# Adding both experts' results of a token in the DRAM row by the indirect store itself

## The chip, the cores and the metric

One core of one Trainium2 chip runs the whole program. The metric is the time on the device in microseconds (us) of one execution; timed runs are taken without the profiler, and beside them one execution was recorded by the hardware profiler. A core has five engines with queues of their own: PE (matrix products; PEld is its weight load), DVE (VectorE), ACT (ScalarE), POOL (GpSimd) and SP (SyncE, which here only issues transfers). Sixteen DMA engines move the data.

## The reference

Sixteen sequences of 256 tokens with 256 features (4096 tokens) go through two layers. What matters here is the last part, the second layer's feed-forward: attention, and then a mixture of eight experts, of which each token takes two.

```python
x = x + o @ w_o + b_o
h = _layernorm(x, ln2_g, ln2_b).reshape(B * S, D)
logits = h @ gate_w + gate_b
topv, topi = jax.lax.top_k(logits, TOPK)            # TOPK = 2
gw = jax.nn.softmax(topv, axis=-1)
ew = jnp.sum(jax.nn.one_hot(topi, E, dtype=h.dtype) * gw[..., None], axis=1)
hid = jax.nn.relu(jnp.einsum('td,edf->etf', h, W1) + b1[:, None, :])
out_e = jnp.einsum('etf,efd->etd', hid, W2) + b2[:, None, :]
moe = jnp.einsum('etd,te->td', out_e, ew)
return x + moe.reshape(B, S, D)
```

Ahead of it stand, in this order: a first layer's mixture of experts (with a shared one), a product-key memory of 4096 experts, and an LSTM over the 256 steps, whose output is the input of the attention. The result of the last part is added to that of the product-key stage.

## The kernel before

The program is one long instruction stream for each engine; a scheduler orders it when the kernel is built, from the dependences between tiles and DRAM tensors, and may move an instruction ahead of others in the source. Each engine runs its own list strictly in that order. There are three stages.

**The first stage** (0 to about 446 us) computes the first layer. Its experts' results go by indirect stores to the DRAM tensor `ayd`, one row for each of a token's two choices. `join` loads both rows of 128 tokens into `r` (L222, on SP), adds them on POOL (L224), turns them by PE (L227) and adds them to `y` on DVE (L229). The last of it overlaps the setup of the next stage: loads of `wx` and `wh` (L973, L974) and of `h0` (L975), scalings of both weights on POOL (L995, L996), memsets.

**The product-key stage** (to about 2345 us) goes over 32 steps `u` of 128 tokens; it has one round more, for the LSTM, which runs one step behind. Each round selects experts on DVE (`select_experts`, which reads `yt`, loaded by L724), builds weights, multiplies by the tables (L839 and L865 on PE) and runs eight LSTM steps (`recur`, L933). `inputs_of` stores the LSTM's inputs to the DRAM tensor `xwd` (L898) and `load_inputs` reads them back (L902). The loads and stores of this stage are on SP.

**The last stage** runs attention of one sequence after another (`front`, `heads`, `ends`) and, interleaved with it by a fixed plan, the experts in 71 tiles of 128 rows (NTL). `ends` finds each token's two experts and sends its row, with the gate and the number of the result's row behind it, to the DRAM tensor `xsd`, in the expert's own region (L1414 on POOL, indirect). The number comes from `dest_i`: choice `c` of token `t` has the number `c * N + t`. After the last sequence, eight `fill` rows of 128 (L1429) close the regions: they have the gate 0 and the numbers from 2N on, a dump of 128 rows.

`experts` then works on tile `n` in three rounds of its loop. `load_tile` loads the rows `xs`, the expert's `w1`, `b1` and `b2` (L1486 to L1495, all on SP). `turn_in` transposes the rows (L1501) and copies them to `xT` (L1503, ACT). `first` is the first product (L1513, PE) with its bias and ReLU in eight pieces, by turns on DVE (L1519) and ACT (L1517). `second` is:

```python
for f in range(NF):
    m = nc.tensor.matmul(acc, hT[n][:, f], mw2[...e...], start=(f == 0), stop=(f == NF - 1))   # L1526
ys = eg.tile([P, D], F32, name="ys", bufs=3)
nc.vector.scalar_tensor_tensor(ys, acc, xs[n][:, D : D + 1], b2[n], ALU.mult, ALU.add)       # L1531
to = eg.tile([P, 1], U32, name="to", bufs=3)
nc.vector.tensor_copy(to, xs[n][:, D + 1 : W].bitcast(U32))                                  # L1533
nc.gpsimd.indirect_dma_start(out=ysd, out_offset=bass.IndirectOffsetOnAxis(ap=to, axis=0), in_=ys, in_offset=None)
```

The last line is L1534: the 128 results go to the rows `to` of the DRAM tensor `ysd`, which has 2N + 128 rows. Nothing in the source says that these stores are independent, so each one waits on POOL for the one before. `to` and `ys` have three buffers each.

After the last attention the tiles that remain follow each other without a break. Eight tiles before the end of the program's loop the source starts to load `base0` to `base7` (L1600 on SP, 512 KB each): the sum so far, kept by `ends` in the DRAM tensor `x3d`. At the end, `ysd` is read back in eight blocks of 512 tokens:

```python
r = jx.tile([P, 2, UB, D], F32, name="r", bufs=4)
for w in range(2):
    at = w * N + c * TBLK
    nc.sync.dma_start(out=r[:, w], in_=ysd[at : at + TBLK].rearrange("(u p) d -> p u d", p=P))   # L1608
nc.vector.tensor_tensor(r[:, 0], r[:, 0], r[:, 1], ALU.add)                                      # L1609
```

Four times two transposes (L1613) and an addition to `base` (L1614) each follow, and the store of the block to `out` (L1615, on ACT's queue).

Of the kernel before, what the change touches and what calls it, by code (L numbers as in the profile page):

```python
# [8 lines left out]
F32 = mybir.dt.float32  # L9
# [3 lines left out]
ALU = mybir.AluOpType  # L13
# [4 lines left out]
P = 128  # L18
B, T, D = 16, 256, 256
N = B * T  # L20
# [13 lines left out]
TBLK = 512  # L34
# [13 lines left out]
def steps(gen, n=None):  # L48

    while n is None or n > 0:  # L50
        if next(gen, gen) is gen:
            return
        n = None if n is None else n - 1
# [108 lines left out]
def adaln_ffn_kernel(ctx: ExitStack, tc: tile.TileContext, i: dict, out: bass.AP):  # L162
    nc = tc.nc
# [3 lines left out]
    ident = const.tile([P, P], F32, name="ident")  # L167
# [7 lines left out]
    pid_i = const.tile([P, 1], mybir.dt.int32, name="pid_i")  # L175
# [15 lines left out]
    I32 = mybir.dt.int32  # L191
# [4 lines left out]
    W = D + 2  # L196
# [41 lines left out]
    with (  # L238
# [70 lines left out]
        dest_i = aw.tile([P, 2, NU], I32, name="dest_i")  # L309
# [260 lines left out]
        with tc.issue_after(marks[1]):  # L570
            nc.scalar.dma_start(out=gam, in_=i["gamma"])
            nc.scalar.dma_start(out=bet, in_=i["beta"])
            for q in range(2):
                w = NE // 2
                nc.scalar.dma_start(out=kin[:, :, q * w : (q + 1) * w], in_=i["kinT"][:, :, q * w : (q + 1) * w])
        with tc.issue_after(marks[2]):
            for q in range(2):
                w = NC // 2
# [55 lines left out]
    NCH = T // SPC  # L634
# [8 lines left out]
    with tc.tile_pool(name="cw", bufs=1) as cw:  # L643
# [8 lines left out]
        dram2 = ctx.enter_context(tc.tile_pool(name="dram2", bufs=1, space=DRAM))  # L652
# [2 lines left out]
        NID = E * (CAP + 1)  # L655
        W = D + 2
        xsd = dram2.tile([(NID + 1) * P, W], F32, name="xsd")
        ysd = dram2.tile([2 * N + P, D], F32, name="ysd")
        x3d = dram2.tile([P, KC, N], F32, name="x3d")
        QC = AH * 32 // P  # L660

# [12 lines left out]
        wh = cw.tile([P, KC, 4, D], F32, name="wh")  # L674
        h0 = cw.tile([P, KC, B], F32, name="h0")
        lnw = fw.tile([P, 4, KC], F32, name="w_ln")
        z0 = fw.tile([P, KC, T], F32, name="z0")
        wqk = fw.tile([P, 2, KC, D], F32, name="wqk")
        with (
# [29 lines left out]
            def tiles_of(c):  # L709
                return slice(c * XT * SPC, (c + 1) * XT * SPC)  # L710
# [3 lines left out]
            def of_tile(ap, u):  # L714
                return ap[:, :, :, u * SPC : (u + 1) * SPC]
# [184 lines left out]
            def load_inputs(v, half):  # L900
                for j in range(CG):
                    nc.sync.dma_start(  # L902
                        out=xr[half][j * CW : j * CW + B],
                        in_=xwd[v].rearrange("(t b) j f -> j b t f", b=B)[j, :, half * HS2 : (half + 1) * HS2],
                    )
# [50 lines left out]
            def new_w():  # L956
                return cx.tile([P, NC, P], F32, name="wts")
# [7 lines left out]
            w = new_w()  # L965
# [15 lines left out]
            for n, gate in enumerate(ORDER):  # L981
                for k in range(KC):
                    at = gate * KC + k
# [26 lines left out]
            def chosen_by(u):  # L1010

                if u < 0:
                    return 0
                return min((NCH - 1) * NS, NS * (u + 1) + min(NS, NS // 4 * u))
# [10 lines left out]
            for u in range(NCH + 1):  # L1025
                if u < NCH:
                    if u % XT == 0:
                        xt[u // XT] = cx.tile([P, KC, B, XT * SPC], F32, name="x1", bufs=2)
                        nc.sync.dma_start(out=xt[u // XT], in_=i["xT"].rearrange("p k (b t) -> p k b t", t=T)[:, :, :, tiles_of(u // XT)])
                    part = of_tile(xt[u // XT], u % XT)  # L1030
                    dense = experts(u, w, part, early if u == 0 else None)

                at, must, to = chosen_by(u - 1), NS * (u + 1), chosen_by(u)
                lead = -(-max(0, must - at) // 2)
                gw = iter(())
                if u + 1 < NCH:
                    w = new_w()
                if u > 0:
                    v = u - 1
                    inputs_of(v, of_tile(xt[v // XT], v % XT))  # L1040
                    load_inputs(v, 0)
                    if v % XT == 0:
                        zt[v // XT] = cx.tile([P, KC, B, XT * SPC], F32, name="zt", bufs=2)
                    back = recur(v, of_tile(zt[v // XT], v % XT))
                NQ = NC // CQ
                for q in range(NQ):
                    if u < NCH:
                        steps(dense, 1)
                    if u + 1 < NCH:
                        if q < lead:  # L1050
                            steps(choices, min(2, must - at))
                            at += min(2, must - at)
                        else:
                            if q == lead:
                                gw = weights_of(done[u + 1], w)
                            n, of = q - lead, NQ - lead
                            steps(gw, (n + 1) * NQ // of - n * NQ // of)
                            more = (to - at) * (n + 1) // of - (to - at) * n // of
                            steps(choices, more)
                    steps(back, 1)  # L1060
                steps(back)
                steps(dense)
                steps(gw)
                if u < NCH and u % XT == XT - 1:
                    nc.sync.dma_start(out=x1d[:, :, :, tiles_of(u // XT)], in_=xt[u // XT])
                if u > 0 and v % XT == XT - 1:
                    nc.gpsimd.tensor_copy(z0[:, :, tiles_of(v // XT)], zt[v // XT][:, :, 0])
                    nc.sync.dma_start(out=zd[:, :, :, tiles_of(v // XT)], in_=zt[v // XT])
# [11 lines left out]
    I32 = mybir.dt.int32  # L1080
    final = ctx.enter_context(ExitStack())
    with (
# [25 lines left out]
        for m in range(2 * HC):  # L1108
            to, at = slice(m * DK, (m + 1) * DK), slice(m % HC * 32, m % HC * 32 + DK)
# [47 lines left out]
            nc.gpsimd.memset(t, 1.0)  # L1157
        fill = fl.tile([P, W], F32, name="fill")
        nc.gpsimd.memset(fill, 0.0)
        nc.vector.tensor_scalar(fill[:, D + 1 : W].bitcast(I32), pid_i, 2 * N, None, ALU.add)  # L1160
        nc.sync.dma_start(out=xsd[NID * P : (NID + 1) * P], in_=fill)
        NPAD = 2
        npads = fl.tile([P, NPAD, NTT, P], F32, name="npads")
# [22 lines left out]
        ecap = fl.tile([P, E], F32, name="ecap")  # L1186
        nc.vector.tensor_scalar(ecap, iota8, float(N + P), None, ALU.mult)
        dest_i = fl.tile([P, 2, N // P], I32, name="dest_i")
        nc.gpsimd.iota(dest_i, pattern=[[N, 2], [P, N // P]], base=0, channel_multiplier=1)

        count = fl.tile([P, E], F32, name="count0")
        nc.vector.memset(count, 0.0)
# [282 lines left out]
        def experts():  # L1475
# [45 lines left out]
            def second(n):  # L1521
                with tc.issue_after(done[n - 2]) if n > 1 else nullcontext():
                    e = nc.tensor.value_load(reg[n][0:1, n : n + 1], min_val=0, max_val=E - 1)
                acc = pg.tile([P, NF // 2, P], F32, name="g", tag="g").rearrange("p f n -> p (f n)")[:, 0:D]
                for f in range(NF):
                    m = nc.tensor.matmul(  # L1526
                        acc, hT[n][:, f], mw2[:, bass.ds(e, 1), f].rearrange("p o d -> p (o d)"), start=(f == 0), stop=(f == NF - 1)
                    )
                done[n] = m.ins
                ys = eg.tile([P, D], F32, name="ys", bufs=3)  # L1530
                nc.vector.scalar_tensor_tensor(ys, acc, xs[n][:, D : D + 1], b2[n], ALU.mult, ALU.add)  # L1531
                to = eg.tile([P, 1], U32, name="to", bufs=3)
                nc.vector.tensor_copy(to, xs[n][:, D + 1 : W].bitcast(U32))  # L1533
                nc.gpsimd.indirect_dma_start(out=ysd, out_offset=bass.IndirectOffsetOnAxis(ap=to, axis=0), in_=ys, in_offset=None)  # L1534

            for n in range(NTL + 2):
                if n < NTL:
                    load_tile(n)
                if 0 <= n - 1 < NTL:
                    turn_in(n - 1)  # L1540
                if n - 2 >= 0:
                    second(n - 2)
                yield
                for half in range(2):
                    if 0 <= n - 1 < NTL:
                        first(n - 1, half)
                    yield
# [45 lines left out]
        UB = 4  # L1593
        jx = final.enter_context(tc.tile_pool(name="jx", bufs=1))
        pj_ = final.enter_context(tc.tile_pool(name="jp", bufs=3, space=PSUM))
        base = []
# [5 lines left out]
        go(NTL * PIECES)  # L1602
        steps(moe)
        for c in range(NBLK):
            r = jx.tile([P, 2, UB, D], F32, name="r", bufs=4)
            for w in range(2):
                at = w * N + c * TBLK
                nc.sync.dma_start(out=r[:, w], in_=ysd[at : at + TBLK].rearrange("(u p) d -> p u d", p=P))  # L1608
            nc.vector.tensor_tensor(r[:, 0], r[:, 0], r[:, 1], ALU.add)  # L1609
            for u in range(UB):  # L1610
                pj = pj_.tile([P, KC, P], F32, name="pj")
                for k in range(KC):
                    nc.tensor.transpose(pj[:, k], r[:, 0, u, k * P : (k + 1) * P], ident)  # L1613
                nc.vector.tensor_tensor(base[c][:, :, u * P : (u + 1) * P], base[c][:, :, u * P : (u + 1) * P], pj, ALU.add)  # L1614
            nc.scalar.dma_start(out=out[:, :, c * TBLK : (c + 1) * TBLK], in_=base[c])  # L1615
# [77 lines left out]
```

## Time and profile before

| What | us |
|---|---|
| timed runs (3): median, lowest, highest | 3600.56, 3600.42, 3603.99 |
| the profiled execution's own time | 3588.3 |
| its span, from the first to the last instruction | 3585.7 |
| PE busy | 3371.2 (94%) |
| DVE busy | 2277.3 (64%) |
| ACT busy | 1494.7 (42%) |
| POOL busy | 682.5 (19%) |
| loads of `r` from `ysd` (L1608): 16 of 512 KB, median from issue to landing | 9.4 |
| additions of the two halves of `r` (L1609): 8, mean of one | 1.22 |
| indirect stores to `ysd` (L1534): 71, median on POOL; median to landing | 1.026; 2.5 |

A line of a timeline gives the start, the duration, the engine, the line of the kernel, the operation, the tiles as written <- read, their shapes and the count; in brackets stands the idle time of the engine just before, and what ended it. An engine name with a q (SPq) is the engine's own queue: the time in which it issues a transfer or waits for a semaphore. "DMA to landing" is counted from the issue to the moment at which the data have landed.

### The profile page before, as it was taken

The numbers are of one execution on the slowest core, as the hardware profiler recorded it, in microseconds if no ns is written. First come the engines' busy times: TensorE is split into PE (matmuls) and PEld (weight loads), VectorE is DVE, ScalarE is ACT, GpSimd is POOL, SyncE is SP. The second block draws the span as 40 slices with busy tenths as digits, with TensorE's granted clock in tenths as the row PEclk, the third lists the DMA queues.
The fourth block names the chain that finished last, engine by engine and source line by source line (L and its number), as shares of the span: only waits on it lengthen the run. The fifth ranks groups of instructions, "written<-read, shape, count | busy, mean of one in ns | idle before, by whom it ended". The sixth has DMA issues, their size and how long they took to land.

```text
span 3585.7 us, 72808 instructions
## 1 busy us (share of the span) xinstructions
PE 3371.2 (94%) x26776; PEld 2563.4 (71%) x26776; DVE 2277.3 (64%) x7358; ACT 1494.7 (42%) x3701; POOL 682.5 (19%) x1164
## 2 busy tenths in 40 slices
PE   8899979999999999999999999969999999999896
PEld 5377557777777777777777777735677777777796
DVE  4333478888878787878888787435555555564323
ACT  1133134545454454545454554334444434443221
POOL 4555210100010100000010100101222222222221
PEclk9899989999999999999999999968999999999997
DMA  6333521111111111011111111130223333333566
GB/s 229 124 103 101 175 41 31 19 34 22 36 24 29 36 23 37 16 37 22 36 22 31 33 23 31 28 120 21 74 92 114 104 117 104 117 102 102 195 216 222
DMA packets 422255, 272.78 MB, mean 76 GB/s; under 512 B 304720, under 2 KB 381136, under 8 KB 411024
## 3 DMA queue, kind: packets, MB, share of 16 engines
q1 hardware_dynamic: 397504, 207.95, 20.9%
q0 software_dynamic: 13344, 36.60, 2.8%
q10 hardware_dynamic: 11056, 23.60, 2.0%
q8 instruction: 216, 3.54, 0.4%
q14 instruction: 135, 1.11, 0.1%
HBM read 191.62 MB, written 76.44 MB: 75 GB/s over the span
## 4 chain that ended last, share of the span: by engine, by line
PE 77%; DVE 9%; ACT 4%; DMA 4%; issue 3%; POOL 2%; SPq 1%; ACTq 0%; DVEq 0%; POOLq 0%
PE acc L865 13%; PE po L839 9%; PE gp L933 7%; PE wp L822 7%; PE g L1526 6%; PE g L1513 6%; PE sc L1277 3%; PE sp L736 3%; PE bp L889 3%; PE ph L529 2%; PE mm L1305 2%; PE py L543 2%; DVE i L747 2%; DVE s L746 1%; PE acc L427 1%
## 5 line engine op out<-in xcount | busy, mean ns | idle before, releaser
L839 PEld LDWEIGHTS po<-yt,kin 128*128 128x128 f32 x3840 | 459.1, 191 | 104.4 <-issue 103.5
L865 PEld LDWEIGHTS acc<-ge,kout 128*128 128x128 f32 x3968 | 466.5, 192 | 85.7 <-DVE ge L862 42.2
L865 PE MATMUL acc<-ge,kout 128*128 128x128 f32 x3968 | 505.3, 280 | 3.1 <-DVE ge L862 1.7
L839 PE MATMUL po<-yt,kin 128*128 128x128 f32 x3840 | 507.0, 281 | 0.0
L826 ACT COPY wts<-wp 64x256 f32<-64x256 f32 x1024 | 375.2, 366 | 180.9 <-PE wp L822 168.2
L952 POOL TENSOR_SCALAR zt<-hT 128x32 f32<-128x32 f32 x256 | 122.4, 478 | 1552.3 <-DVE hT L951 1437.9
L933 PE MATMUL gp<-wh,hT 128*32 128x256 f32 x4096 | 318.3, 393 | 31.1 <-DVE hT L951 20.8
L817 DVE TENSOR_TENSOR oh<-chosen,parted 128x1024 f32<-128x1024 f32 x256 | 311.9, 1218 | 0.0
L822 PE MATMUL wp<-oh,ol 128*64 128x128 f32 x4096 | 297.4, 281 | 5.7 <-ACT wts L826 5.1
L1517 ACT ACTIVATE hT<-g,b 128x128 f32<-128x128 f32 x284 | 104.7, 369 | 423.9 <-DVE hT L1519 370.6
L1526 PE MATMUL g<-mw,hT 128*128 x1136 | 273.2, 396 | 5.6 <-ACT xT L1503 3.1
L1513 PE MATMUL g<-xT,w 128*128 128x128 f32 x2272 | 274.4, 276 | 1.0 <-DVE ys L1531 1.0
L1513 PEld LDWEIGHTS g<-xT,w 128*128 128x128 f32 x2272 | 269.0, 192 | 5.6 <-DVE ys L1531 1.2
L822 PEld LDWEIGHTS wp<-oh,ol 128*64 128x64 f32 x4096 | 226.6, 137 | 57.7 <-issue 12.8
L1526 PEld LDWEIGHTS g<-mw,hT 128*128 128x128 f32 x1136 | 221.3, 200 | 42.0 <-ACT xT L1503 8.1
L843 ACT ACTIVATE ge<-po 128x512 f32<-128x512 f32 x248 | 147.2, 594 | 200.7 <-PE po L839 194.7
L933 PEld LDWEIGHTS gp<-wh,hT 128*32 128x32 f32 x4096 | 118.7, 110 | 155.0 <-issue 50.3
L814 DVE TENSOR_TENSOR ol<-chosen,iota 128x512 f32<-128x512 f32 x256 | 174.9, 683 | 66.8 <-ACT chosen L798 47.1
L939 ACT ACTIVATE g<-gp 128x192 f32<-128x192 f32 x256 | 84.8, 331 | 286.6 <-PE gp L933 285.1
L1277 PE MATMUL sc<-qk 32*128 32x256 f32 x2048 | 192.2, 412 | 8.6 <-DVE npads L1284 7.2
L862 DVE TENSOR_TENSOR ge<-ge,wts 128x512 f32<-128x512 f32 x248 | 169.3, 683 | 38.8 <-ACT ge L843 29.6
L1519 DVE TENSOR_SCALAR hT<-g,b 128x128 f32<-128x128 f32 x284 | 96.8, 341 | 130.5 <-PE g L1513 76.6
(354 smaller groups left out, 5390.6 us busy)
## 6 DMA issues: line engine op xcount, KB each, us to landing
w<-in_mw SPq DMA_DIRECT2D x71, 1024.0 KB, 5.0
xwd<-xw SPq DMA_DIRECT2D x64, 256.0 KB, 3.8
xr<-xwd SPq DMA_DIRECT2D x256, 64.0 KB, 2.5
xs<-axd SPq DMA_DIRECT2D x71, 129.0 KB, 2.2
xs<-xsd SPq DMA_DIRECT2D x71, 129.0 KB, 2.1
b<-in_b SPq DMA_DIRECT2D x71, 128.0 KB, 4.4
r<-ayd SPq DMA_DIRECT2D x64, 128.0 KB, 2.7
mw<-in_mw SPq DMA_DIRECT2D x8, 1024.0 KB, 14.9
```

Source lines behind the costliest of these rows:

```text
L814: nc.vector.tensor_tensor(ol, bc(c[:, 0, g : g + GT], 2, NK), bc(iota[:, 0:NK], 1, GT), ALU.is_equal)
L817: nc.vector.tensor_tensor(oh, bc(c[:, 1, g : g + GT], 2, P), bc(parted, 1, GT), ALU.is_equal)
L822: nc.tensor.matmul(wp[half[s], t], ol[:, at, :], oh[:, at, :], start=True, stop=True)
L826: nc.scalar.copy(wr[half[h], :, :, at : at + GH], wp[half[s], :, :, h * NHI : (h + 1) * NHI].rearrange("p t r c -> p c r t"))
L839: nc.tensor.matmul(po[:, h, :].rearrange("p (b t) -> p b t", t=SPC), kin[:, k, (c + h) * P : (c + h + 1) * P], yu[:, k], start=(k == 0), s ...
L843: nc.scalar.activation(to, po, AF.Gelu)
L862: nc.vector.tensor_tensor(ge, ge, w[:, c : c + CQ, :], ALU.mult)
L865: nc.tensor.matmul(acc[d], kout[:, c + h, d * P : (d + 1) * P], ge[:, h, :], start=(c + h == 0), stop=(c + h == NC - 1))
L933: nc.tensor.matmul(gp[j * CW : (j + 1) * CW], state["hT"][:, k, :], group(wh, k, j), start=False, stop=(k == KC - 1), skip_group_check=True,)
L1277: nc.tensor.matmul(s[j][:, t], qk[rows(j), w, c, t * P : (t + 1) * P], qk[rows(j), 1 - w, c, :], start=True, stop=True)
L1513: nc.tensor.matmul(ph[:, f], w1[n][:, k, at * P : (at + 1) * P], xT[n][:, k], start=(k == 0), stop=(k == KC - 1))
L1526: m = nc.tensor.matmul(acc, hT[n][:, f], mw2[:, bass.ds(e, 1), f].rearrange("p o d -> p (o d)"), start=(f == 0), stop=(f == NF - 1))
```

## The change

The number of a result's row becomes the token's number for both choices, and the indirect store adds to what the row holds instead of writing over it. `ysd` shrinks to N + 128 rows. Because the rows must start at zero, a zeroed tile `none` is stored to all 33 blocks of 128 rows, in the rounds of the product-key stage (34 stores, since the block of the dump is written twice). The last stage loads one row a token, and the addition on DVE is gone.

```diff
-        ysd = dram2.tile([2 * N + P, D], F32, name="ysd")
+        ysd = dram2.tile([N + P, D], F32, name="ysd")
...
+        none = cw.tile([P, D], F32, name="none")
+        nc.gpsimd.memset(none, 0.0)
...
                 steps(gw)
+
+                for q in range(u, min(u + 1, NCH) if u < NCH - 1 else N // P + 1):
+                    nc.sync.dma_start(out=ysd[q * P : (q + 1) * P], in_=none)
...
-        nc.vector.tensor_scalar(fill[:, D + 1 : W].bitcast(I32), pid_i, 2 * N, None, ALU.add)
+        nc.vector.tensor_scalar(fill[:, D + 1 : W].bitcast(I32), pid_i, N, None, ALU.add)
...
-        nc.gpsimd.iota(dest_i, pattern=[[N, 2], [P, N // P]], base=0, channel_multiplier=1)
+        nc.gpsimd.iota(dest_i, pattern=[[0, 2], [P, N // P]], base=0, channel_multiplier=1)
...
-                nc.gpsimd.indirect_dma_start(out=ysd, out_offset=bass.IndirectOffsetOnAxis(ap=to, axis=0), in_=ys, in_offset=None)
+                nc.gpsimd.indirect_dma_start(
+                    out=ysd, out_offset=bass.IndirectOffsetOnAxis(ap=to, axis=0), in_=ys, in_offset=None, compute_op=ALU.add
+                )
...
-            r = jx.tile([P, 2, UB, D], F32, name="r", bufs=4)
-            for w in range(2):
-                at = w * N + c * TBLK
-                nc.sync.dma_start(out=r[:, w], in_=ysd[at : at + TBLK].rearrange("(u p) d -> p u d", p=P))
-            nc.vector.tensor_tensor(r[:, 0], r[:, 0], r[:, 1], ALU.add)
+            r = jx.tile([P, UB, D], F32, name="r", bufs=4)
+            nc.sync.dma_start(out=r, in_=ysd[c * TBLK : (c + 1) * TBLK].rearrange("(u p) d -> p u d", p=P))
             for u in range(UB):
                 pj = pj_.tile([P, KC, P], F32, name="pj")
                 for k in range(KC):
-                    nc.tensor.transpose(pj[:, k], r[:, 0, u, k * P : (k + 1) * P], ident)
+                    nc.tensor.transpose(pj[:, k], r[:, u, k * P : (k + 1) * P], ident)
```

In the changed kernel the indirect store is L1539, the zero stores are L1068, the loads of `r` L1613 and the loads of `base` L1607; L1513 and L1526 of the two products become L1518 and L1531.

## The prediction

> **What bounds the kernel now.** I read the page first, then the chain of waits by window, the windows of the end, and then the rows of the lines that the diff edits. The page says that PE is busy for 94% of the span and that the busy share of the DMA engines is low except at the two ends:
>
> ```profile
> span 3585.7 us, 72808 instructions
> ...
> PE   8899979999999999999999999969999999999896
> ...
> DMA  6333521111111111011111111130223333333566
> ```
>
> So nothing that is only moved between idle queues in the middle can be worth much. The diff works in three places: the front of the product-key stage (about 437 to 546 us), the stores of the experts (2597 to 3542 us), and what follows the last expert tile. The chain of waits from 3544 us on, and the windows of the same stretch (columns: window, length, busy time of PE, PEld, DVE, ACT, POOL, granted clock, DMA share, GB/s):
>
> ```profile
> by line: DMA r<-ysd 40.8%; DMA out<-base 15.9%; DVE base L1614 11.1%; DVE r L1609 8.8%; DMA ysd<-ys,to 5.8%; PE pj L1613 4.8%; SPq L1608 3.3%; issue 2.8%; DVEq L1609 0.2%
> ...
> 3544.00:3550.00 6.00, 0.00 (x0) 0.00 (x0) 0.00 (x0) 0.00 (x0) 0.00 (x0) 0.55 0.65 210
> ...
> 3560.00:3565.00 5.00, 3.06 (x14) 2.16 (x12) 4.12 (x9) 0.00 (x0) 0.00 (x0) 0.50 1.07 392
> ...
> 3570.00:3575.00 5.00, 1.94 (x8) 1.51 (x8) 3.80 (x6) 0.00 (x0) 0.00 (x0) 0.50 1.08 384
> ...
> 3580.00:3586.00 6.00, 1.19 (x6) 0.73 (x4) 1.63 (x4) 0.00 (x0) 0.00 (x0) 0.50 0.26 100
> ```
>
> The last 40.85 us (first `r` load at 3544.85, end at 3585.7) are bound by transfers: all 16 engines are busy and move about 385 GB/s, PE idles at half clock.
>
> **The end.** Sixteen loads of 0.524 MB and eight stores of 0.524 MB make 12.58 MB; eight loads go, 4.19 MB. Bytes alone: 4.19 MB / 385 GB/s = 10.9 us less. That is the small end. In proportion to the bytes, 40.85 x 8/12 = 13.6 us less. Rebuilt step by step: the fastest `r` load landed 4.0 us after its issue, of which 0.524 MB / 385 GB/s = 1.4 us is transfer, so 2.6 us of dead start; then 8.39 MB / 385 GB/s = 21.8 us; then about 0.9 us to the last landing, 25.3 us in all, 15.5 less. The compute doesn't get in the way: eight `r` additions (L1609, 1.22 us each, in front of the transposes of their block) are gone, and a block is 1.94 us of transposes over 1.7 us of DVE additions, 8 x 1.94 = 15.5 us after a first landing of 4.0 and before a store of 5.5 us, about 25 us too. Only four `r` buffers exist, but a block gives its own back after 1.94 us. I take 26.5 us, a gain of 14.3 us, with 10.9 and 15.5 as ends.
>
> **The adding store.** It is the unknown. The 71 stores of today:
>
> ```profile
> L1534 POOL DMA_INDIRECT ysd<-ys,to x71: 961/1026/1055, 2597.5 to 3542.4; - x71
> L1534 POOLq EVENT_SEMAPHORE  x70: 17/17/3072, 2611.4 to 3537.9; - x70
> ...
>   DVE to L1533: 19.4, 27
> ...
> DMA to landing us min/median/max: 2.4/2.5/5.8
> ```
>
> POOL already waits for the previous store before each next one (70 semaphore waits, median 17 ns), so the order that the additions need is paid; between stores lie 7.24 us at the least. Call L the time from a store's start on POOL to its landing. Low end: 2.45 us, as now. High end by the rows: the destination rows have to be read first, and the nearest read of 129 KB from DRAM, `xs<-xsd`, lands in 2.1 us: 2.45 + 2.1 = 4.6 us. No row forbids that it becomes slower still, which is rival B. I take the middle, 3.5 us. POOL's own 1.03 us may grow as well, and is in L.
>
> The Trainium skill, "Collectives: The Full Stack", section "The bandwidth ceiling: the fold count and why AG ≠ RS ≠ AR", speaks against the change: it says that an addition inside a DMA costs a second read descriptor for each chunk and halves the rate (32.35 against 62.28 GB/s there). As an estimate, doubling the 0.34 us that 0.131 MB take at the measured 385 GB/s would make L 2.8 us, and the sum below 0.7 us better.
>
> What waits for L? First the end: the last store landed 2.4 us after 3542.41 and the first `r` load waits for it, so L - 2.45 falls wholly on the path: +1.05 us (0 to 2.1). Second, DVE's copy `to` (L1533): it has three buffers, is run three tiles ahead, and so waits for the store just issued; behind it in DVE's queue stand the last ReLUs of a tile, which PE's L1526 needs. In the steady part:
>
> ```profile
> 3490.88 3.73 PE L1513 MATMUL g<-xT,w 128*128 128x128 f32 x32
> ...
> 3494.41 0.15 DVE L1533 COPY to<-xs 128x1 uint32<-128x1 uint32 x1 [0.36 <-DMA ysd<-ys,to]
> ...
> 3494.65 0.35 DVE L1519 TENSOR_SCALAR hT<-g,b 128x128 f32<-128x128 f32 x1
> ...
> 3494.67 3.62 PE L1526 MATMUL g<-mw,hT 128*128 x16
> ```
>
> How much later may `to` come? The trace has a test: while `base` was being loaded the stores landed late.
>
> ```profile
> 3384.06 3.72 PE L1526 MATMUL g<-mw,hT 128*128 x16 [0.52 <-ACT xT L1503]
> ...
> 3385.16 0.15 DVE L1533 COPY to<-xs 128x1 uint32<-128x1 uint32 x1 [2.51 <-DMA ysd<-ys,to]
> ...
> 3416.99 0.15 DVE L1533 COPY to<-xs 128x1 uint32<-128x1 uint32 x1 [1.83 <-DMA ysd<-ys,to]
> ```
>
> At 3385.16 it came 1.10 us after L1526 began, and L1526 took 3.72 us as always. In the steady part L1526 begins about 2.75 us after POOL starts the store, so no stall is due up to L = 2.75 + 1.2 = 3.95 us. The order of DVE's instructions, the same in both kernels, has `to` between the second and third ReLU in 12 tiles from 3419 us on; in three tiles before, it stands later and bears about 4.9 us (the row at 3416.99 came 4.92 us after its store, and cost PE 0.3 us). The price is 12 x (L - 3.95) and 3 x (L - 4.9), where positive. With L = 3.5 it is nothing; with 4.6 it is 7.8 us. Among the attention tiles (before 3365 us) `to` waits for `ysd` only 2.8 us in all, since the stores lie further apart: nothing there.
>
> **Zeroing.** 34 stores of 0.131 MB, 4.46 MB, all on SP. The source puts them in 33 rounds; the order of the built kernel has them all on SP between the first loads of the stage and the first `xwd` store. Before:
>
> ```profile
> 469.47 5.17 SPq L724 DMA_DIRECT2D yt<-yd  x2
> ...
> 545.88 0.35 SPq L898 DMA_DIRECT2D xwd<-xw  x1
> ```
>
> SP is idle from 474.6 to 545.9 us and the DMA engines moved 1 to 2 GB/s from 480 to 545 us. 34 issues of about 0.4 us are 14 us; the bytes at 233 GB/s (440 to 460 us) are 19 us; both end by about 500 us. Without that cover it would be these 19 us. One zero store slips in front of the first `yt` load (about 0.6 us); its reader on DVE at 474.24 us had 3 us to spare. Price 0. The 0.24 us memset on POOL, and the two `wx` scalings that now stand before the last two additions of the join, may make the last join 2.7 us later, but DVE then waits anyway, until 453.49 us, for `h0`. I take 0, with -1 to +2 as ends.
>
> **One load moved.** In the built order the first `base` load stands ahead of the `xs` load of the first tile after the fills, not three tiles later. SP issues it in 0.6 us, and `xs` then lands behind 0.524 MB (1.4 us). PE is idle for just this `xs`:
>
> ```profile
> 3365.00 0.66 PE L1501 MATMUL g<-ident,xs 128*128 128x128 f32 x2 [5.66 <-DMA xs<-xsd]
> ```
>
> Part of the 1.4 us passes while SP still waits for the last fill (landed 3362.6). I take +1.2 us, between 0 and +2.2. The weights behind it (issued at 3363.4, 5.0 us to landing, read by L1513 at 3371.4) have 3 us to spare.
>
> **Sum.** -14.3 + 1.05 + 0 + 0 + 1.2 = -12.05 us. The profiled execution took 3588.3 us (span 3585.7 and 2.6 around it), so 3576.2 us under the profiler; the three timed runs have the median 3600.56, 12.3 us above it, and I carry the difference over: 3588.5 us. A measurement can tell about 0.2%, 7.2 us, from no change.
>
> **Rivals.** A (the forecast): L below 4.3 us; -7.2 is reached where 13 L = 55.75. 60%.
> C: L between 4.3 and 5.3 us: the end gains, 12 tiles give it back; -7 to +7 us, 3593 to 3608, about 3600. For it: the row bound of 4.6 us lies in it. Against: it supposes that read and write follow each other without overlap. 18%.
> B, the other side: the store with addition takes over as the bound of the steady tiles through `to`. It decides from L = 4.85 us (gain zero) and is slower by 7.2 us from L = 5.3; at 6.5 us it is 16 x 6.5 - 77.65 = +26 us, 3627. For it: plain stores have landed in up to 5.8 us under load, and no row shows an adding one. Against: in the steady part they land in 2.5. 20%.
> D: the last stage gains nothing, because eight stores and the transposes are its bound. The eight stores alone are 10.9 us and the transposes 15.5 us of 40.85, so this is excluded almost wholly; 3600 to 3603. 2%.
>
> **Numbers.** Faster 0.59 (A, less the corner where the end gives only 10.9), same 0.19 (C, D and that corner), slower 0.22. Range 3585.3 (end at 15.5, L as now) to 3612 (B up to L = 5.6); A by itself is 3585 to 3593.
>
> **What would show it.** Right: `r<-ysd` x8, the end 25 to 28 us after the first `r` load at about 385 GB/s; L1539 landing below 4 us; L1526 and L1513 still at 3.46 and 3.6 us in turn from 3410 to 3535. Wrong: `to` waiting over 1.5 us a tile and PE waiting for ReLUs, a period above 7.24 us; or POOL's instruction well above 1.03 us; or PE waiting for `xs` by more than 7 us near 3365.

## The result, and the profile after

The changed kernel is slower: a median of 3618.21 us in 12 runs (3609.34 to 3638.68), beside 3599.99 us for the kernel before in 12 runs beside them. The ratio is 1.0058, with a 95% interval from 1.0041 to 1.0075, so +15 to +27 us. Executions of one kernel differ by 19 to 33 us with the clock that PE is granted (of the kernel before in 29 other runs, the fastest took 3581.57 us at a mean clock of 0.966 and the slowest 3614.64 at 0.955); so stretches are compared below between landmarks inside one profile, and whole times by ratios.

The page of the changed kernel, the same rows as were shown of before:

```profile
span 3616.5 us, 72815 instructions
...
PE   8899879999999999999999999779999999999897
...
DMA  7333531101110111101111110221233333333576
```

PE is busy for 94% of the span as before, and the page doesn't say where 30.8 us of span went. (The medians of the timed runs lie 18.2 us apart, less than these two profiles.) Landmarks of the two profiles do (start of the first and last store to `ysd`, of the first `fill` store, of the first `r` load):

| stretch | before | after | difference |
|---|---|---|---|
| start to first `ysd` store | 2597.5 | 2598.4 | +0.9 |
| first store to first `fill` (tiles beside the attention) | 754.8 | 782.2 | +27.4 |
| first `fill` to last store (tiles without attention) | 190.1 | 204.25 | +14.15 |
| last store to first `r` load (its landing) | 2.44 | 3.80 | +1.36 |
| first `r` load to the end | 40.85 | 27.85 | -13.0 |
| sum | | | +30.8 |

So the end gained what it was meant to gain, and the two stretches of the expert tiles lost three times as much. The windows of the end (columns as before), and the chain of waits from 3588 us on:

```profile
3590.00:3595.00 5.00, 2.31 (x11) 2.16 (x12) 1.60 (x4) 0.00 (x0) 0.00 (x0) 0.50 0.99 332
...
3600.00:3605.00 5.00, 1.98 (x11) 1.25 (x10) 2.29 (x7) 0.00 (x0) 0.00 (x0) 0.85 1.07 394
...
by line: DMA r<-ysd 50.4%; PE pj L1617 24.7%; DMA ysd<-ys,to 13.2%; DVE base L1618 5.9%; issue 1.1%
```

The DMA engines are full from 3590 to 3610 us, and the loads of `r` are half of the chain. But a quarter of it are the transposes of `r` (L1617): the fifth to the eighth load wait until a transpose gives a buffer back, and are issued 6.0 to 10.4 us after the first. The answer for the line of the store:

```profile
L1539 POOL DMA_INDIRECT ysd<-ys,to x71: 1569/1602/1652, 2598.4 to 3584.9; - x71
...
  DVE to L1538: 66.8, 42
...
DMA to landing us min/median/max: 3.6/3.8/8.6
```

An adding store takes 1.60 us on POOL instead of 1.03 and lands after 3.8 us instead of 2.5, and DVE's copy `to` waits 66.8 us for it instead of 19.4. Where these waits lie is the point. First, one tile beside the attention, before:

```profile
2768.47 1.04 POOL L1534 DMA_INDIRECT ysd<-ys,to  x1 [0.16 <-DVE qk L1290]
...
2771.64 0.15 DVE L1533 COPY to<-xs 128x1 uint32<-128x1 uint32 x1
...
2774.51 0.88 DVE L1341 SCALAR_TENSOR_TENSOR z<-mm,w_bo,z 128x256 f32<-128x256 f32 x2 [1.63 <-PE mm L1339]
...
2777.42 1.74 DVE L1219 RECIPROCAL rs<-rs 128x256 f32<-128x256 f32 x1
```

and the same tile after:

```profile
2776.10 1.62 POOL L1539 DMA_INDIRECT ysd<-ys,to  x1 [0.15 <-issue]
...
2779.86 0.15 DVE L1538 COPY to<-xs 128x1 uint32<-128x1 uint32 x1 [1.11 <-DMA ysd<-ys,to]
...
2781.31 0.88 DVE L1346 SCALAR_TENSOR_TENSOR z<-mm,w_bo,z 128x256 f32<-128x256 f32 x2 [0.17 <-PE mm L1344]
...
2785.31 1.75 DVE L1224 RECIPROCAL rs<-rs 128x256 f32<-128x256 f32 x1 [1.00 <-ACT rs L1223]
```

Before, `to` came 3.17 us after the start of its store and found it landed; the row has no bracket at all. After, DVE arrives 2.65 us after the store and waits 1.11 us; the ReLUs behind `to` go late to ACT, ACT's `rs` is late, and DVE and PE wait for that a second time (the last row for DVE). Before, 22 of the 45 copies of `to` that the profile records beside the attention came 2.50 to 3.65 us after their store: a landing at 3.84 us would make these 22 late by 19.1 us in sum, and the wait for `ysd` there did rise by 19.8 us (from 2.8 to 22.6).

Second, the burst of `base` loads behind the fills, after:

```profile
3409.50 1.60 POOL L1539 DMA_INDIRECT ysd<-ys,to  x1 [4.12 <-DVE ys L1536]
3409.63 1.18 SPq L1607 DMA_DIRECT2D base<-x3d  x2
3413.05 1.99 PE L1531 MATMUL g<-mw,hT 128*128 x8 [0.52 <-ACT xT L1508]
3418.24 0.15 DVE L1538 COPY to<-xs 128x1 uint32<-128x1 uint32 x1 [6.61 <-DMA ysd<-ys,to]
3418.71 3.39 PE L1531 MATMUL g<-mw,hT 128*128 x8 [3.67 <-DVE hT L1524]
```

With two loads of 0.5 MB behind it the store lands after 8.6 us; PE stops for 3.67 us in the middle of L1531, and the eight products after the gap take 3.39 us where the eight before it took 1.99.

Third, the last tiles, on which the prediction had spent its care, are untouched: from store 55 to store 70 it is 108.5 us before and 109.2 after, though `to` waits in each of them:

```profile
3471.21 3.62 PE L1531 MATMUL g<-mw,hT 128*128 x16
...
3472.24 0.15 DVE L1538 COPY to<-xs 128x1 uint32<-128x1 uint32 x1 [1.65 <-DMA ysd<-ys,to]
```

### The profile page after: what moved, and what is told of

It is laid out like the page before. It is cut to its first block, busy times and chain, and to the rows that moved or that the text cites. A ratio compares the mean times of both kernels' runs of the same rounds, so it can differ in the third digit from the quotient of the medians.

```text
span 3616.5 us, 72815 instructions
## 1 busy us (share of the span) xinstructions
PE 3387.2 (94%) x26776; PEld 2574.5 (71%) x26776; DVE 2266.9 (63%) x7350; ACT 1493.5 (41%) x3701; POOL 727.8 (20%) x1165
## 3 DMA queue, kind: packets, MB, share of 16 engines
q14 instruction: 135, 1.11, 0.1%
## 4 chain that ended last, share of the span: by engine, by line
PE 67%; DVE 11%; DMA 6%; issue 6%; ACT 5%; POOL 3%; SPq 1%; ACTq 0%; POOLq 0%; DVEq 0%
PE acc L867 13%; PE po L841 9%; PE gp L935 7%; PE wp L824 7%; PE g L1531 4%; PE sp L738 3%; PE bp L891 3%; PE g L1518 3%; DMA ysd<-ys,to 2%; PE sc L1282 2%; PE ph L529 2%; PE py L543 2%; DVE i L749 1%; PE mm L1310 1%; DVE s L748 1%
## 5 line engine op out<-in xcount | busy, mean ns | idle before, releaser
L1531 PE MATMUL g<-mw,hT 128*128 x1136 | 279.4, 402 | 20.3 <-DVE hT L1524 7.8
L1518 PE MATMUL g<-xT,w 128*128 128x128 f32 x2272 | 275.9, 277 | 0.0
L1518 PEld LDWEIGHTS g<-xT,w 128*128 128x128 f32 x2272 | 270.9, 193 | 4.8 <-issue 0.3
L1531 PEld LDWEIGHTS g<-mw,hT 128*128 128x128 f32 x1136 | 224.2, 203 | 60.0 <-ACT xT L1508 10.5
L935 PEld LDWEIGHTS gp<-wh,hT 128*32 128x32 f32 x4096 | 118.7, 110 | 155.6 <-issue 50.3
```

What stands on the lines that cost most here:

```text
L935: nc.tensor.matmul(gp[j * CW : (j + 1) * CW], state["hT"][:, k, :], group(wh, k, j), start=False, stop=(k == KC - 1), skip_group_check=True,)
L1518: nc.tensor.matmul(ph[:, f], w1[n][:, k, at * P : (at + 1) * P], xT[n][:, k], start=(k == 0), stop=(k == KC - 1))
L1531: m = nc.tensor.matmul(acc, hT[n][:, f], mw2[:, bass.ds(e, 1), f].rearrange("p o d -> p (o d)"), start=(f == 0), stop=(f == NF - 1))
```

## The experiments

Theory S: the loss is DVE standing at `to` until the adding store has landed. Rival P: POOL's longer instructions delay what others need from POOL. Rival Q: the zeroing and the moved `base` load. The stretches of all runs, from their profiles (us), and the timed ratio to the kernel before, run beside it:

| kernel | store 0 to `fill` | `fill` to last store | last store to `r` | `r` to end | ratio, 95% interval |
|---|---|---|---|---|---|
| before | 754.8 | 190.1 | 2.4 | 40.85 | |
| after | 782.2 | 204.2 | 3.8 | 27.85 | 1.0058 [1.0041, 1.0075] |
| e1 after, 8 `to` buffers | 757.8 | 193.4 | 3.8 | 28.6 | 0.9982 [0.9962, 1.0002] |
| e12 after, 4 `to` buffers | 759.9 | 192.4 | 3.8 | 28.5 | 0.9978 [0.9955, 1.0000] |
| e2 before, 8 `to` buffers | 755.8 | 192.3 | 2.4 | 41.0 | 0.9988 [0.9968, 1.0008] |
| e3 after, plain store | 756.8 | 191.3 | 2.4 | 28.2 | 0.9968 [0.9950, 0.9985] |
| e4 before, adding store | 780.4 | 200.3 | 3.9 | 40.6 | 1.0081 [1.0053, 1.0110] |
| e5 after, `to` behind `ys` | 744.3 | 193.0 | 3.9 | 28.0 | 0.9926 [0.9908, 0.9943] |
| e7 before, `to` behind `ys` | 744.6 | 190.1 | 2.4 | 40.9 | 0.9960 [0.9941, 0.9979] |
| e6 after, `base` one a tile | 781.2 | 204.2 | 3.7 | 28.3 | 1.0086 [1.0063, 1.0109] |
| e11 after, `to` behind `ys` from tile 44 | 772.2 | 192.1 | 3.8 | 28.5 | 1.0023 [1.0004, 1.0041] |
| e8 before, zeroing (one run) | 761.9 | 192.5 | 2.4 | 40.4 | |
| e10 before, zeroing | 756.8 | 192.7 | 2.4 | 40.5 | 1.0003 [0.9986, 1.0021] |
| e9 after, `to` behind `ys`, `base` one a tile | 740.8 | 190.1 | 3.7 | 27.9 | 0.9920 [0.9896, 0.9944] |

Stretches that nothing should change scatter (before, e2, e3, e8 and e10: 754.8 to 761.9 and 190.1 to 192.7), so differences of up to 7 us in the first column and of 2 or 3 us in the second carry nothing.

**e1: the wait taken away.**

```diff
-                to = eg.tile([P, 1], U32, name="to", bufs=3)
+                to = eg.tile([P, 1], U32, name="to", bufs=8)
```

> The changed kernel with eight buffers for `to` instead of three; the order of every engine's instructions stays as it is. Theory S (the adding store lands 1.3 us later, and this is paid where DVE's copy `to` waits for its buffer with attention work and ReLUs queued behind it): the waits of L1538 for `ysd` go from 66.8 us to nearly 0, the last store starts about 40 us earlier than in the changed kernel, and the time is 8 to 16 us below the kernel before (end -13, last landing +1.3, moved `base` load +1). Rival P (POOL: 0.57 us more for each store and 0.57 us more for the scaling behind it, 71 times, delays what DVE and PE need from POOL): the waits of `to` go as well, but the time stays within 5 us of the changed kernel, 13 to 31 us above the kernel before. Rival Q (zeroing and the moved `base` load): no change against the changed kernel.

Nothing waits for the store any more, and 35 of the 41.6 us between first and last store are gone (986.5 to 951.2), with the same store of 1.60 us on POOL. The ratio says 6.5 us below the kernel before (from 14 below to 1 above): five buffers of 4 bytes a partition take the loss away, though no gain over the kernel before is shown. The order of the instructions on PE, DVE, POOL and SP is the same in both traces. P and Q fall as the main cause.

**e12: how many buffers.**

```diff
-                to = eg.tile([P, 1], U32, name="to", bufs=3)
+                to = eg.tile([P, 1], U32, name="to", bufs=4)
```

> The changed kernel with four buffers for `to` instead of three, order as it is. Theory S: `to` then waits for the store before the one just issued, which has landed 7.24 us ago less 3.8 us, so the stalls are gone as with eight buffers: 3 to 16 us below the kernel before; only the burst of `base` loads (landings up to 8.6 us) may still bite for 1 to 3 us. If the number of buffers needed were larger (a chain of late stores), 5 us or more above the time with eight.

One buffer more does what five do, although stores of this run landed later still: one after 10.5 us in the burst, and those of tiles 54 to 66 after 5.5 to 7.4 us. With three, `to` waits for the store just issued; with four for the one before it.

**e2: the same in the kernel before.**

```diff
-                to = eg.tile([P, 1], U32, name="to", bufs=3)    # kernel before
+                to = eg.tile([P, 1], U32, name="to", bufs=8)
```

> The kernel before with eight buffers for `to`. Theory S: its 19.4 us of waits for `ysd` go; most of them lay beside other work, so 0 to 5 us faster, most of it between 3365 and 3410 us where `base` is loaded. Rivals P and Q: the same time, within 2 us.

No gain can be seen: 4 us by the ratio, but the interval takes in zero, and the stretches are no shorter than before's. The 19.4 us of waits of the kernel before were covered; the burst, where I looked for the gain, gave none.

**e3: the addition left out.**

```diff
-                    out=ysd, out_offset=..., in_=ys, in_offset=None, compute_op=ALU.add
+                    out=ysd, out_offset=..., in_=ys, in_offset=None
```

> The changed kernel with a plain indirect store in place of the adding one, and nothing else changed; it leaves out the addition of the two experts' results (the later store of a token wins). Theories S and P alike: POOL's instruction is 1.03 us again and lands in 2.5 us, the waits of `to` fall to about 20 us, and the time is 10 to 15 us below the kernel before. Rival Q: the loss stays, 10 us or more above the kernel before, since zeroing, the moved load and the one row a token are all still there.

With zeroing, moved load and one row a token all in place, but a plain store, it is 11.5 us faster than before (5 to 18). Q falls: without the adding store there is no loss.

**e4: the adding store alone.**

```diff
+        none = cw.tile([P, D], F32, name="none")
+        nc.gpsimd.memset(none, 0.0)
...
-                nc.gpsimd.indirect_dma_start(out=ysd, out_offset=..., in_=ys, in_offset=None)
+                nc.gpsimd.indirect_dma_start(out=ysd, out_offset=..., in_=ys, in_offset=None, compute_op=ALU.add)
...
+                for q in range(2 * u, min(2 * u + 2, 2 * N // P + 1) if u < NCH - 1 else 2 * N // P + 1):
+                    nc.sync.dma_start(out=ysd[q * P : (q + 1) * P], in_=none)
```

> The kernel before with only the store made an adding one, into 2N+128 rows that 65 zero stores clear in the product-key stage; two loads a block and the DVE additions stay, and the first `base` load stays where it was. Theories S and P: the whole loss without the gain of the end, 25 to 45 us above the kernel before, first `r` load 25 to 45 us later than 3544.85. Rival Q: under 8 us above it (twice the zero stores, no moved load).

+29 us by the ratio (19 to 40), with the loss in the same two stretches (+25.6 and +10.2) and the end as long as before.

**e5 and e7: `to` put where it waits for nothing.**

```diff
+                made = nc.vector.scalar_tensor_tensor(ys, acc, xs[n][:, D : D + 1], b2[n], ALU.mult, ALU.add)
...
-                nc.vector.tensor_copy(to, xs[n][:, D + 1 : W].bitcast(U32))
+                with tc.issue_after(made.ins):
+                    nc.vector.tensor_copy(to, xs[n][:, D + 1 : W].bitcast(U32))
```

> The changed kernel with three `to` buffers as it is, but DVE's copy `to` is put right behind `ys` of its own tile; PE, ACT and SP keep their order. It then waits neither for the store just issued nor for an early `xs`. Theory S (the loss is DVE standing at `to`): as with eight buffers, first to last store about 950 us instead of 986.5, the time 5 to 15 us below the kernel before; if the 100 us that DVE waits at `to` for `xs` also cost PE time, up to 10 us more. Rival P (POOL's longer instructions are the loss): no change against the changed kernel, about 18 us above the kernel before.

> The kernel before with `to` put right behind `ys` in the same way. Theory S: what eight buffers gave (about 4 us), and if waiting for `xs` at `to` costs PE time, as much again as it gives the changed kernel: 2 to 14 us faster. Rival P: the same time, within 2 us.

The answers of the profile for the line of `to`, in the changed kernel and in e5 (the list under the second line names what DVE waited for; in e5 it is empty):

```profile
its engine sat idle before it (us, times) until:
  DMA xs<-xsd: 112.0, 27
  DMA ysd<-ys,to: 66.8, 42
```

```profile
L1539 DVE COPY to<-xs x71: 133/144/151, 2612.0 to 3550.4; 128x1 uint32<-128x1 uint32 x71
its engine sat idle before it (us, times) until:
```

e5 is 27 us below the kernel before (20 to 33), past what I expected of the store's wait alone; e7 is 14 us below it. Since eight buffers gave the kernel before nothing (e2), its gain here points to the other wait at `to`, that for an early `xs`: beside the attention the stretch is about 10 us shorter (744.6 against 754.8). That the wait alone does it isn't shown, since with the copy moved POOL's order changes too (in both kernels a scaling on POOL, `b` or `row`, goes ahead of a store in 14 places). Between e5 and e7, which share the moved copy, lie 11.4 us (medians 3587.09 of six runs and 3598.47 of five, each scattered over 11 to 12 us): with `to` out of the way, the change brings about what the prediction had summed to 12.05. P falls here too: up to the first `fill` POOL is busy for 234.1 us in e5 and 206.6 us in e7, and both take 744 us.

**e6: the `base` loads spread.**

```diff
+                now["got"] = got
...
-            nc.sync.dma_start(out=t, in_=x3d[:, :, c * TBLK : (c + 1) * TBLK])
+            with tc.issue_after(now["got"][54 + c]):
+                nc.sync.dma_start(out=t, in_=x3d[:, :, c * TBLK : (c + 1) * TBLK])
```

> The changed kernel with the eight `base` loads one a tile, each behind the `xs` load of tile 54 to 61, instead of in a burst behind the fills (tiles 46 to 53). Theory S: the 13 us that the changed kernel loses between stores 46 and 53 come from landings of 5 to 8.6 us in the burst; one load a tile stretches a landing by 1.4 us (0.5 MB at 385 GB/s) to about 5.2 us at most, 1.2 us over the 3.95 that the order bears, so 5 to 10 us of it are won, and the time is 8 to 14 us above the kernel before. Rival R (the 13 us are the slow clock after the wait for `xs`, not the stores): they stay, about 18 us above the kernel before.

My size was wrong: nothing is won. Waits and chain of e6 between 3440 and 3520 us, and 3440 and 3480 us:

```profile
DVE to L1539 <- DMA ysd<-ys,to: 28.6, 9, 3.7
...
PE g L1532 <- DVE hT L1525: 10.6, 8, 1.6
```

```profile
3450.82 5.56 DMA ysd<-ys,to
...
3456.41 0.15 DVE to L1539
```

In the eight tiles that have a load beside them `to` now comes 5.2 to 5.8 us after its store, and the next store comes 8.6 to 9.2 us after the last one instead of 7.24. In each of the eight the delay is what `to` is late beyond 3.91 us (5.24 and 8.57, 5.59 and 8.92, 5.83 and 9.16 us); together it is 12.8 us, about what the burst had cost (13.0 between stores 46 and 53, of which 1.1 is the moved load). So the prediction's threshold of 3.95 us, which it had read off the kernel before, is confirmed to 0.04 us in its own place. R falls: with the loads moved, stores 46 to 53 take 64.3 us instead of 75.3 (62.3 before), and the eight tiles lose theirs at the full clock.

**e11: only the late tiles.**

```diff
+                made = nc.vector.scalar_tensor_tensor(ys, acc, xs[n][:, D : D + 1], b2[n], ALU.mult, ALU.add)
...
+                with tc.issue_after(made.ins) if n >= 44 else nullcontext():
+                    nc.vector.tensor_copy(to, xs[n][:, D + 1 : W].bitcast(U32))
```

> The changed kernel with `to` put behind `ys` from tile 44 on only; the tiles beside the attention keep their order. Theory S: the last tiles run as in the pinned kernel, first store to first fill stays at about 781 us (755 before), so 25 to 27 us of loss remain and about 13 go: 0 to 8 us above the kernel before. If the forecast's view of the attention tiles (nothing there) held, it would be as fast as the fully pinned one, 27 us below the kernel before.

8 us above the kernel before (1 to 15). At store 42 it stands at 734.1 us from the first, as the changed kernel does (735.2; before 714.1): the 20 us of the attention tiles are still lost, and behind the fills all is back (192.1 us). (The copies run up to three tiles ahead, so moving those from tile 44 on already tells between store 42 and the fills: 38.1 us against 47.0. That is why the stretch is 772 and not 781.)

**e8 and e10: zeroing alone.** The tile `none` is made as in e4.

```diff
+                for q in range(2 * u, min(2 * u + 2, 2 * N // P + 1) if u < NCH - 1 else 2 * N // P + 1):
+                    nc.sync.dma_start(out=ysd[q * P : (q + 1) * P], in_=none)
```

> The kernel before with 65 zero stores to `ysd` in the product-key stage and nothing else (plain stores, two loads). Theories S and P: the zeroing hides, nobody waits for it, the last stage from first to last store is 945 to 949 us as before. Rival Q (zeroing costs): PE is idle by 5 us or more beyond the kernel before around 450 to 550 us.

> The kernel before with 65 zero stores and nothing else, timed. Theory S: within 4 us of the kernel before (the one run of it, 3638 us, was late by a low clock between 2345 and 2600 us, not by the zeroing). Rival Q: 10 us or more above the kernel before.

The single run e8 took 3638.32 us, above every run of the kernel before beside it (highest 3625.3). Its first store came at 2638 us, but no instruction waited for a zero store in it, and between 2345 and 2600 us PE's clock was 0.69 (0.84 before, 0.76 in e10). Twelve runs of the same kernel (e10) settle it: 1.0003, within 8 us of nothing, for 65 zero stores. Why the clock was low there in that run stays open.

**e9: both edits.** The changed kernel with the edits of e5 and e6.

> The changed kernel with both edits: `to` right behind `ys`, and the eight `base` loads one a tile behind the `xs` of tiles 54 to 61. If the moved `base` load is what is left of the loss (between stores 46 and 47 the pinned changed kernel is 2.6 us behind the pinned kernel before), first to last store comes to about 935 us instead of 937.3, and the time is about 2 us below that of the pinned changed kernel, 25 to 33 us below the kernel before. Landings stretched by the `base` loads to 5.2 us and more cost nothing now. If they still stall PE (theory S wrong on where), tiles 53 to 61 take 8.8 us each again and it is 10 us or more slower than the pinned one.

20 to 37 us below the kernel before (24.6 by the medians), the lowest ratio of all, though not told apart from e5's. Its landings, and the longest wait of PE between 3352 and 3545 us (no wait for a store or a ReLU is left among them):

```profile
DMA to landing us min/median/max: 3.7/3.9/7.5
```

```profile
PE g L1507 <- DMA xs<-xsd: 6.1, 1, 6.1
```

Stores still land late beside the `base` loads, and nobody stands behind them; the tiles keep their 7.24 us. The stretch behind the fills is 2.9 us shorter than in e5, about the size I expected, but no larger than the scatter.

## Why the prediction was wrong

It forecast 3588.5 us and faster; it became 3618.21 and slower. By its own steps:

- **The end**, -14.3: measured -13.0, between its ends. The rate was read too high: the windows from 3590 to 3600 us moved 332 GB/s, not 385, and before, those from 3550 to 3560, which the prediction didn't show, had moved 354 and 349. "The compute doesn't get in the way" holds only in part, since four of the eight loads waited for a buffer; whether that cost anything while the DMA engines were full stays open. (In the prediction's proportion 40.85 x 8/12 is 27.2 us, the time that is left, and 13.6 us is the gain.)
- **The adding store's landing**, L = 3.5: measured 3.8 us, inside its bounds; the last landing cost +1.36 where +1.05 was put. The rule of the Trainium skill ("Collectives: The Full Stack", "The bandwidth ceiling: the fold count and why AG ≠ RS ≠ AR"), stated there for the rings of collectives, pointed the right way, but the estimate of 2.8 us from it was low: the packets of queue 0, which carries the indirect stores, take 4.2% of 3616.5 us of all 16 engines now and took 2.8% of 3585.7, 0.73 us more for each store rather than 0.34, and the landing came 1.3 us later.
- **The stalls at `to`, priced at 0: the step that failed**, in the sentence "Among the attention tiles ... `to` waits for `ysd` only 2.8 us in all, since the stores lie further apart: nothing there". A wait that is small today says how late the store is today, not how much later it may become. The copies came 2.50 to 3.65 us after their stores, with margins of 0 to 1.2 us; by this row L = 3.5 would have made them late by 11.8 us in sum and 3.84 by 19.1. The stretch lost 27.4 us. It is this wait and not another that the loss hangs on: with more buffers (e1, e12) or with a plain store (e3) it is gone, with the adding store alone (e4) it is there, and with only the late copies moved (e11) the part beside the attention stays.
- **The `base` burst**: the step used three tiles that "bear about 4.9 us" and left L there at the steady 3.5. But plain stores had already landed after 4.0 to 4.9 us in that burst, and adding ones take up to 8.6. Priced at 0, it cost 10.2 us in e4, where the first `base` load is not moved.
- **The steady tiles**: the bound of 3.95 us held (3.91 in e6), and L = 3.8 cost them 0.7 us in 15 tiles. That was near to luck: `to` came 3.7 to 3.9 us after its store there, and the one that came after 4.49 us paid 0.59 us.
- **The moved load**, +1.2 (0 to 2.2): held. From the issue of the last `fill` store to the transpose that needs `xs` it is 4.3 to 4.9 us in the eight profiles without the load in front (before, e2, e4, e6 to e10; 4.6 on average) and 5.3 to 7.4 us in the six with it (after, e1, e3, e5, e11, e12; 6.1); between before and after it is 1.0 us.
- **Zeroing**, 0: held (+0.9 to the first store; e10).

Rival B named the mechanism and the sign, but let it decide from L = 4.85 us and in the steady tiles; it decided at 3.8, in the tiles before them, beside the attention and in the burst. Most of the prediction's signs of being right came true in a kernel that was slower (eight loads of `r`, the end 27.85 us after the first of them, a landing of 3.8 us): they looked at the end and at the steady tiles alone.

Of the 27.4 us beside the attention only half is PE standing still:

```profile
2597.50:3352.30 754.80, 717.45 (x5618) 589.41 (x5617) 420.53 (x1163) 319.49 (x663) 206.81 (x300) 0.98 0.32 108
```

```profile
2598.40:3380.60 782.20, 730.57 (x5617) 599.59 (x5616) 420.83 (x1163) 317.28 (x663) 235.92 (x299) 0.96 0.35 104
```

PE is idle for 14.3 us more (51.6 against 37.3) and busy for 13.1 us more with the same matmuls, at a granted clock of 0.96 instead of 0.98. The clock records fit that: PE is at half clock for 64.9 us of this stretch after and for 34.1 before, and half of the difference, which is what it costs at most, is 15.4 us. In the other two kernels that add and keep the order (e4, e6) PE is idle for 50.3 and 52.3 us and at half clock for 64.9 in both; in e11 for 46.0 and 58.0; in the ten others for 31.6 to 41.0 and 34.1 to 44.4. One place shows the step: before, PE waits 1.10 us for ACT's `rs` at 2846.5 and 1.72 us at 2849.1, and is at half clock for 3.41 us from 2851.6 on; after, the wait for `rs` at 2854.9 is 1.86 us long, the next at 2858.3 is 1.71 us, and the half clock lasts 6.83 us from 2859.4 on. That the gaps lower the clock was not tried by itself.

## What to carry to other kernels

Before an asynchronous operation is made slower, list the start of each instruction that waits for its completion, minus the start of the operation: the smallest of these margins in every stage is what may be added, and a wait that reads zero can be a margin of zero. Look at what else loads the DMA queues where the margin is used. And a copy that a scheduler hoists ahead of its need, into few buffers, puts its wait in front of everything behind it: put it right before its reader, or give it one buffer more.

## What the runs showed of the hardware

- An adding indirect store of 128 rows of 1 KB took 1.60 us on POOL (plain 1.03) and landed after 3.8 us (plain 2.5; medians of the 41 and 33 stores whose landing the profiles show). With two loads of 0.5 MB behind it, it took up to 8.6 us, in e12 10.5; plain ones took up to 4.9 in that burst and 5.8 at most.
- Where the expert's weight load of 1 MB was issued 2.7 us after the store, as in the steady tiles after, the adding store landed after 3.7 to 4.5 us; where it was issued between 1.0 us before and 1.1 us after the store (e11 and e12, tiles 54 to 66), after 5.4 to 7.6.
- POOL's scaling `b` right behind an adding store is recorded with 1.51 us instead of 0.94, but it starts 1.08 us after the store's start in both kernels and so overlaps it: the two together take 2.58 us instead of 2.01 (medians), 0.57 more and not twice that.
- A stall of PE came with a second price, its clock: after the gap of 3.67 us shown above eight products took 3.39 us instead of 1.99, and from 3410 to 3464 us the granted clock was 0.91, where the same tiles before (3380 to 3434 us) had 1.00. The Trainium skill, "TensorE: Matmul & The Clock Gate", section "HAM oscillation — how this bites in real kernels", gives about 3.4 us of idle as the length from which the clock is halved; this row agrees, but it isn't the least: the clock was also halved at 2851.6 us before, where the longest wait just ahead was 1.72 us and PE had been busy for 1.69 of the last 3.44 us. In e6, eight waits of 1.1 to 1.7 us, one a tile, left it at full speed.
